# A decoder layer on one core: transposes of q, k and dequantised weight rows taken from TensorE and given to VectorE and the stores

## The chip, the core and the metric

The kernel runs on one core of a Trainium2 chip, in one launch. Its time is the device time in microseconds (us), the median of several runs. TensorE is called PE in the profile (PEld is its weight load), VectorE DVE, ScalarE ACT, GpSimd POOL, and SyncE, which here only issues DMAs, SP.

## The reference

A post-norm decoder layer over 8 batches of 256 tokens, width 1024, float32. Each of three sublayers is added to its input and normalised.

```python
# 1: causal attention, 32 heads of 32, 8 key/value heads
qkv = x @ w_qkv
xq, xk = rope(xq), rope(xk)          # pairs (x1, x2) -> (x1 cos - x2 sin, x1 sin + x2 cos)
probs = softmax(mask(xq @ xk.T / sqrt(32)));  out = (probs @ xv) @ w_o
# 2: cross-attention to ctx_4096, one head of 1024
Q = h @ Wq.T + bq;  K = ctx @ Wk.T + bk;  out = softmax(Q @ K.T / 32) @ ctx
# 3: a linear layer whose weight is dequantised: 4 (or 8) bit planes -> code -> table row
w_l = take_along_axis(lut4, code4, axis=1);  w_h = take_along_axis(lut8, code8, axis=1)
y = where(norm(x) > 64, x @ w_h.T, x @ w_l.T) + bias
```

## The kernel before, in words

All work is in tiles of 128 partitions. Most matrix products run as seven block products per batch (`winograd`), with the sums of blocks made by DVE or POOL. The program has three stages, and on PE, DVE, ACT and POOL every instruction keeps the order in which the Python code issues it (class `InOrder`; all of them carry line 59 in the profile). DMAs written as `nc.sync.dma_start` go to SP's one queue in an order that a scheduler sets when the kernel is built, those written as `sync.dma_start` in the order of the program.

**Stage 1 (`front(b)`, lines 581 to 675).** For each batch, q (four accumulators of 128 tokens x 512 columns) and k, v (256 columns each) are multiplied. A loop over steps (28 for a batch, 32 for the first) sets the order: one half product a step, q and k/v in turn. A finished accumulator is handed to `rotate` (line 543): four DVE multiplications over the even or the odd elements write `ra` and `rb`, POOL adds them (line 559), and five steps later `turn` (line 561) transposes `ra` on PE in 128x128 blocks into a PSUM bank (tag `tp`, two banks) and ACT copies the bank into `q_t` or `k_t`, q scaled by 1/sqrt(32). At the end of a batch q_t, k_t and v are stored to DRAM (`keep_q`, `keep_kv`).

**The dequantisation (`dequant_low`, line 340)** is a generator beside this, 64 blocks of 128 rows x 128 columns, five steps each. In a block DVE masks bit plane 0 (`first`) and makes it 0 or 1, masks planes 1 to 3 (`m`); ACT makes eight leaves `t` out of the table; DVE selects between them in three predicated copies, the last two of them one block later (`finish`), and the 128x128 result is stored to `wr_d`, 64 stores. Line 661 sets how many of the 320 steps are done in stage 1: 240. The others are done in stage 2, three in a visit.

**Stage 2 (lines 678 to 922).** 48 visits, six a batch, and three more to drain: scores, softmax and values of a group of heads, in portions, PE work of four different visits overlapping (`LAG = 3`). Beside the visits, four portions in each, runs a chain of other work (`Beside`): the output projection of the batch before (15 steps), the product of the two cross-attention weights (`weight_product`, 24 pieces of two steps, which begins at the end of stage 1), and in batches 5 and 6 `weights_turned(4)`, 8 steps each: `transpose_weights` (line 402) loads rows of `wr_d` (tile `row`), PE transposes them, ACT copies the bank to `stage`, and a store writes `wf_d`. `run(low)` (line 891, visit 33) finishes the dequantisation. In its last eight pieces `weight_product` also stores a column of 128 single elements to `u_d`, loads a row block of wk into `wide` (tag `row`, two buffers, shared with the rows above) and reduces it on DVE (line 472). The tag `m` (two buffers) is shared by the pieces' results and `stage`.

**Stage 3 (lines 926 to 1115).** Cross-attention and the linear layer; it loads `wf_d` in four quarters (`quads`, line 261) when the last projection lets go of the buffers.

Of the kernel before, what the change touches and what calls it, by code (L numbers as in the profile page):

```python
# [24 lines left out]
F32 = mybir.dt.float32  # L25
BF16 = mybir.dt.bfloat16
I32 = mybir.dt.int32
# [35 lines left out]
def decoder_layer(  # L63
# [67 lines left out]
    wr_d = dram.tile([KC, P, D], F32, name="wr_d")  # L131
    wf_d = dram.tile([2, 2, P, 4, 512], F32, name="wf_d")
    u_d = dram.tile([D], F32, name="u_d")
# [127 lines left out]
    def quads(pool, src, tag, width=512):  # L261

        t = [pool.tile([P, 4, width], F32, name=f"{tag}{i}", tag=f"{tag}{i}") for i in range(7)]
        for i in (0, 2, 1, 3):
            sync.dma_start(t[i], src[i // 2, i % 2])
        return t
# [72 lines left out]

    def dequant_low(pool, bits, lut, width=P):  # L340


        words = width // 32
        last = None

        def finish(n):
            if last is None:
                return
            t, m, to = last
            if n == 1:  # L350
                select(t, m[:, 0:1, :], 1)
            else:
                select(t, m[:, 1:2, :], 2)
                select(t, m[:, 2:3, :], 3)
                nc.sync.dma_start(to, t[:, 0, :])

        for oi in range(KC):
            qw, lt = table(pool, oi, 4, lut, 2)
            diff = pool.tile([P, 8], F32, tag="diff", name="diff", bufs=2)
            dve.tensor_tensor(diff, lt[:, :, 1], lt[:, :, 0], ALU.subtract)  # L360
            for i in range(0, D, width):
                part = slice(i // 32, i // 32 + words)
                first = pool.tile([P, 1, words, 32], I32, tag="first", name="first")
                first = planes_of(qw[:, 0:1, part], bits, first)
                first = first[:, 0]
                one = first.bitcast(F32)
                dve.tensor_scalar(one, first, 0, None, ALU.not_equal)
# [12 lines left out]
                yield  # L380
                finish(2)
                last = t, m, wr_d[oi, :, i : i + width]
                yield
        finish(1)
        finish(2)
# [42 lines left out]
    def weight_product():  # L428
        bq_bc = m_pool.tile([P, D], F32, name="bq_bc")
        nc.sync.dma_start(bq_bc, bq.partition_broadcast(P))  # L430
        wide = dq.tile([P, D], F32, tag="row", name="wide", bufs=2)
        nc.sync.dma_start(wide, bk.partition_broadcast(P))
# [15 lines left out]
        for k, (n, i) in enumerate(pieces):  # L448
# [13 lines left out]
            if k + 2 < len(pieces):  # L462
                loaded.append(load(*pieces[k + 2]))
            m = m_pool.tile([P, 512], F32, tag="m", name="m", bufs=2)[:, :third]
            act.copy(m, ps)
            nc.sync.dma_start(m_d[i, :, ts(n, third)], m)
            if n == 2:
                u = D - 2 * third
                nc.sync.dma_start(u_d[ts(i, P)].rearrange("(p o) -> p o", o=1), m[:, u : u + 1])
                wide = dq.tile([P, D], F32, tag="row", name="wide", bufs=2)  # L470
                nc.sync.dma_start(wide, wk_t[ts(i, P), :])
# [18 lines left out]
    def low_steps(n):  # L490
        for _ in range(n):
            next(low, None)

    def put_low(oi, tp, half):
        stage = m_pool.tile([P, 512], F32, tag="m", name="stage", bufs=2)
        act.copy(stage, tp)
        to = wf_d[half, oi // 4, :, :, ts(oi % 4, P)]
        nc.sync.dma_start(to, stage.rearrange("p (q o) -> p q o", q=4))

    low_turned = transpose_weights(dq, put_low)  # L500


# [30 lines left out]

    cs = f_pool.tile([P, NST, 48], F32, name="cs", bufs=1)
    nc.sync.dma_start(cs, rope.rearrange("(s p) a -> p s a", p=P))
    for i in (1, 3):
# [4 lines left out]
    nc.sync.dma_start(bits, bit)  # L541

    def rotate(acc, st, jn, to):

        n = HD * 4 * jn
        pairs = acc[:, :n].rearrange("p (r j i two) -> p r j i two", r=4, j=jn, two=2)

        order = "p (j r i two) -> p r j i two" if jn == 4 else "p (r j i two) -> p r j i two"
        ra = f_pool.tile([P, n], F32, tag=f"ra{jn}", name="ra", bufs=3 if jn == 4 else 2)
        rb = f_pool.tile([P, n], F32, tag=f"rb{jn}", name="rb", bufs=1)  # L550
        pa, pb = (t[:, :n].rearrange(order, r=4, j=jn, two=2) for t in (ra, rb))
        cos, nsin, sin = (
            cs[:, st : st + 1, None, ts(i, 16)].to_broadcast([P, 4, jn, 16]) for i in range(3)
        )
        dve.tensor_tensor(pa[..., 0], pairs[..., 0], cos, ALU.mult)
        dve.tensor_tensor(pa[..., 1], pairs[..., 1], cos, ALU.mult)
        dve.tensor_tensor(pb[..., 0], pairs[..., 1], nsin, ALU.mult)
        dve.tensor_tensor(pb[..., 1], pairs[..., 0], sin, ALU.mult)
        pool_e.tensor_tensor(ra[:, :n], ra[:, :n], rb[:, :n], ALU.add)

        def turn():
            tp = bank(p_tp, "tp")
            for j in range(jn):
                transpose(tp[:, ts(j, P)], ra[:, ts(j, P)], ident)
            tp = tp[:, :n].rearrange("p (j s) -> p j s", j=jn)

            act.mul(to, tp, 1.0 / HD**0.5 if jn == 4 else 1.0)

        later.append((step + 5, turn))
# [11 lines left out]
    def front(b):  # L581
        n_kv = NKV * HD
        k_t = f_pool.tile([P, 2, S], F32, tag="k_t", name="k_t", bufs=1)
        v = f_pool.tile([P, NST, NKV * HD], F32, tag="v", name="v", bufs=1)
        q_t = [f_pool.tile([P, 4, S], F32, tag=f"q_t{jb}", name="q_t", bufs=1) for jb in range(2)]
        acc = {}
# [11 lines left out]
        def finish_q(st, half):  # L598
            rotate(acc[st, half], st, 4, q_t[half][:, :, ts(st, P)])

        def put_kv(st, half, ps):
            n = NKV * HD
            if half:
                act.copy(v[:, st, :], ps[:, :n])
                return
            acc[st] = f_pool.tile([P, n], F32, tag="acc_k", name="acc_k")
            act.copy(acc[st][:, :n], ps[:, :n])
            if st == 1:
                rotate(acc[st], st, 2, k_t[:, :, ts(st, P)])

        def add_kv(st, half, ps):
# [3 lines left out]
            if not half:  # L615
                rotate(acc[st], st, 2, k_t[:, :, ts(st, P)])

# [5 lines left out]
        def whole_kv(st, half, ps):  # L623
            put_kv(st, half, ps)
            if (st, half) == (0, 0):
                rotate(acc[0], 0, 2, k_t[:, :, :P])

        def keep_q():
            for jb in range(2):
                nc.sync.dma_start(q_d[b][jb], q_t[jb])  # L630

        def keep_kv():
            nc.sync.dma_start(k_d[b], k_t)
            nc.sync.dma_start(v_d[b], v)

        def kept(steps, keep):
            yield from steps
            later.append((step + 5, keep))

# [4 lines left out]
        else:  # L644
# [3 lines left out]
            kv_steps = classical(p1, a, (raw_kv[0:2], raw_kv[2:4]), n_kv, whole_kv, "uv")  # L648
        yield from in_turn(kept(q_steps, keep_q), kept(kv_steps, keep_kv))

# [4 lines left out]
    for b in range(B):  # L655
        for n, _ in enumerate(front(b), 1):
# [3 lines left out]

            while low_done * (steps - 20) < 240 * (step - 20):
                low_steps(1)
                low_done += 1
# [8 lines left out]
    for _, f in later:  # L672
        next(product)
        f()
    s1_stack.close()

# [137 lines left out]

    def weights_turned(n):
        for _ in range(2 * n):
            next(low_turned, None)
            yield

    mw = []  # L820
# [48 lines left out]
    for k in range(len(visits) + LAG):  # L869
# [14 lines left out]
        if k >= EACH and k % EACH == LAG and b < B:  # L884
# [5 lines left out]
            if b == 5:  # L890
                run(low)
            if 5 <= b <= 6:
                parts.append((weights_turned(4), 8))
            beside = Beside(4 * EACH, *parts)
# [264 lines left out]
def _rope_table(np):  # L1159
# [5 lines left out]
    cos, sin = np.cos(angles), np.sin(angles)  # L1165
    return np.concatenate([cos, -sin, sin], axis=1).astype(np.float32)

# [53 lines left out]
```

## Time and profile before

| | us |
|---|---|
| median of 3 runs | 1531.33 (1527.86 to 1533.06) |
| the profiled execution, its own time | 1527.34 |
| its span, first to last instruction | 1525.3 |
| busy: PE / DVE / ACT / POOL | 1407.2 / 993.7 / 661.6 / 510.3 |
| mean granted TensorE clock | 0.979 |
| DMA | 69755 packets, 153.06 MB; 12944 packets under 512 B |

The profile is one execution. A row of a table of stretches gives, for a stretch of the span, each engine's busy time with its number of instructions, the granted TensorE clock (1.00 is full speed), the mean busy share of the 16 DMA engines and GB/s. A row of waits gives the engine and tile that waited, what ended the wait, and the total time, the number and the longest. A row of a tile gives the shortest, median and longest duration of its instructions in ns. In a timeline, a row is a start, a length, an engine and an operation, with the number of instructions merged into it.

### The profile page before, as it was taken

How to read it: one execution, taken by the hardware profiler on the slowest of the kernel's cores; microseconds unless marked ns; L12 is line 12 of the kernel's file. 1: busy time of each engine (PE TensorE's matmuls, PEld its weight loads, DVE VectorE, ACT ScalarE, POOL GpSimd, SP SyncE). 2: the span in 40 equal slices, each digit the busy share in tenths (PEclk: the TensorE clock that was granted, in tenths of full speed). 3: DMA queues.
4: the chain of work that ended last, by engine and by line, in shares of the span. 5: the costliest groups of instructions: out<-in, count | busy, mean ns of one | idle time of the engine just before them, and what ended most of it. 6: DMA issues, size and time to landing. Idle time of an engine off the chain costs nothing. (4 is left out here: it accounts for less than half of the span.)

```text
span 1525.3 us, 20159 instructions
## 1 busy us (share of the span) xinstructions
PE 1407.2 (92%) x7314; PEld 884.5 (58%) x7314; DVE 993.7 (65%) x1579; ACT 661.6 (43%) x2028; POOL 510.3 (33%) x304
## 2 busy tenths in 40 slices
PE   8899899898899999989979789999999999999996
PEld 4555555555455555455545444885867667685842
DVE  3977778683988889987655674345455464545462
ACT  1556566662688787776545662012111011202110
POOL 2623323220745354443424352064133131404112
PEclk9999999999999999999988999999999999999999
DMA  9222112215641216061463345421222122131211
GB/s 332 74 82 84 57 39 89 81 52 194 237 174 62 100 42 159 24 152 58 104 145 100 115 135 195 150 84 42 98 77 89 56 83 69 70 111 39 73 41 44
DMA packets 69755, 153.06 MB, mean 100 GB/s; under 512 B 12944, under 2 KB 32400, under 8 KB 67216
## 3 DMA queue, kind: packets, MB, share of 16 engines
q1 hardware_dynamic: 69648, 151.70, 30.7%
q8 instruction: 60, 0.98, 0.3%
q14 instruction: 47, 0.39, 0.1%
HBM read 101.33 MB, written 50.34 MB: 99 GB/s over the span
## 5 line engine op out<-in xcount | busy, mean ns | idle before, releaser
L59 POOL TENSOR_TENSOR pr<-pr,rsum 128x1024 f32<-128x1024 f32 x96 | 187.3, 1952 | 284.7 <-DVE rsum L59 246.0
L59 ACT ACTIVATE t<-first,lt,diff 128x128 f32<-128x128 f32 x512 | 206.0, 483 | 98.4 <-DMA wr_d<-t 45.5
L59 ACT ACTIVATE pr<-pr,nm 128x256 f32<-128x256 f32 (+1 forms) x512 | 226.0, 446 | 41.0 <-DVE rsum L59 22.3
L59 DVE COPY_PREDICATED t<-m,t 128x512 f32<-128x512 int32 (+2 forms) x192 | 156.1, 813 | 3.2
L59 PEld LDWEIGHTS tp<-ident,pr 128*128 128x128 f32 x800 | 94.1, 143 | 106.2 <-issue 77.0
L59 PE MATMUL tp<-ident,pr 128*128 128x128 f32 x800 | 125.2, 284 | 25.8 <-ACT pt L59 19.3
L59 DVE TENSOR_TENSOR pr<-sc,causal 128x1024 f32<-128x1024 f32 x96 | 115.9, 1208 | 48.3 <-PE sc L59 34.3
L59 POOL TENSOR_TENSOR ra<-ra,rb 128x512 f32<-128x512 f32 (+1 forms) x48 | 63.7, 1327 | 242.4 <-DVE rb L59 238.8
L59 DVE TENSOR_REDUCE nm<-pr 128x4 f32<-128x1024 f32 (+1 forms) x96 | 117.1, 1220 | 3.3
L59 PE MATMUL x<-wq,xt 128*128 128x512 f32 x200 | 98.9, 618 | 16.9 <-ACT acc L59 10.3
L59 ACT COPY pt<-tp 128x512 f32<-128x512 f32 (+1 forms) x144 | 74.7, 554 | 79.3 <-PE tp L59 79.2
L59 POOL TENSOR_TENSOR sf<-h_t 128x512 f32<-128x512 f32 x8 | 10.2, 1271 | 288.1 <-DVE h_t L59 275.7
L59 ACT ACTIVATE sd<-mv,eps 128x1 f32<-128x1 f32 (+2 forms) x34 | 10.0, 295 | 220.9 <-DVE mv L59 220.9
L59 ACT ACTIVATION_READ_ACCUMULATOR pr<-pr,nm 128x1 f32 x512 | 97.6, 191 | 0.0
L59 PE MATMUL x<-w,o_t 128*128 128x512 f32 x192 | 89.7, 594 | 0.8 <-DVE h L59 0.8
L59 DVE TENSOR_TENSOR h<-x,h 128x512 f32<-128x512 f32 x64 | 44.0, 687 | 65.7 <-PE x L59 58.1
L59 PE MATMUL x<-w,h_t 128*128 128x512 f32 x192 | 86.3, 592 | 0.0
L59 ACT COPY h_t<-tp 128x512 f32<-128x512 f32 x32 | 18.7, 584 | 128.6 <-PE tp L59 128.6
L59 PE MATMUL tp<-pt,v 128*32 128x256 f32 (+1 forms) x640 | 63.2, 435 | 10.9 <-DVE pt L59 5.6
L59 DVE TENSOR_TENSOR h<-z,h 128x512 f32<-128x512 f32 x48 | 33.0, 687 | 59.0 <-PE z L59 57.6
L59 DVE COPY pt<-tp 128x512 f32<-128x512 f32 x64 | 43.2, 676 | 43.1 <-PE tp L59 43.0
L59 PE MATMUL x<-wk,wq 128*128 128x342 f32 x192 | 62.1, 469 | 6.0 <-ACT t L59 4.1
(144 smaller groups left out, 2741.1 us busy)
## 6 DMA issues: line engine op xcount, KB each, us to landing
h_d<-h SPq DMA_DIRECT2D x32, 512.0 KB, 3.4
wq<-in_wq SPq DMA_DIRECT2D x24, 512.0 KB, 5.2
xt<-in_x_t SPq DMA_DIRECT2D x32, 256.0 KB, 4.4
q_d<-q_t SPq DMA_DIRECT2D x16, 512.0 KB, 3.1
q_t<-q_d SPq DMA_DIRECT2D x16, 512.0 KB, 6.0
h<-in_x SPq DMA_DIRECT2D x16, 512.0 KB, 6.7
h<-h_d SPq DMA_DIRECT2D x16, 512.0 KB, 4.0
ct_b<-in_c_t SPq DMA_DIRECT2D x8, 1024.0 KB, 4.8
```

The costliest lines, as they stand in the source:

```text
L59: return lambda *args, **kw: self.tc.keep_in_program_order(issue(*args, **kw))
```

## The change

`rotate` makes two wide multiplications on DVE, over a table that holds each cosine and sine twice (a reversed read swaps the pairs), and a scaled table `cs_q` takes the place of the scaling on ACT. POOL adds as before. `turn` is a DVE transpose, which transposes each 32x32 square of the tile by itself into `turned` (two buffers), and four stores, one for each group of 32 partitions, place the squares in `q_d` or `k_d` in runs of 32 floats (128 B). The tiles q_t and k_t of stage 1 and their stores at the end of a batch are gone.

In the dequantisation, the plane 0 mask is made for two blocks at once; a finished block is transposed in squares by DVE, and after every second block four stores place the squares in `wf_d`, whose layout gets the group of 32 as an inner dimension. `wr_d`'s use for this, `put_low`, `weights_turned` and its loads, PE transposes and copies are gone. 210 steps are done in stage 1 where 240 were. `wide` has one buffer, `m` is as wide as its pieces, and the four loads of `wf_d` are sixteen, of 32 partitions each.

```diff
-    wf_d = dram.tile([2, 2, P, 4, 512], F32, name="wf_d")
+    wf_d = dram.tile([2, 2, 32, 4, 4, 512], F32, name="wf_d")
...
+            for c in range(4):
+                sync.dma_start(t[i][ts(c, 32)], block[:, :, c])
...
-                nc.sync.dma_start(to, t[:, 0, :])
+                oi, i = to
+                if i % 256 == 0:
+                    rows.append(pool.tile([P, 2, 4, 32], F32, tag="turned", name="turned", bufs=2))
+                dve.transpose(rows[-1][:, i // P % 2].rearrange("p c o -> p (c o)"), t[:, 0, :])
+                if i % 256:
+                    q = i // P % 4 - 1
+                    for a in range(4):
+                        o = P * (oi % 4) + 32 * a
+                        nc.sync.dma_start(
+                            wf_d[i // 512, oi // 4, :, q : q + 2, :, o : o + 32],
+                            rows[-1][32 * a : 32 * a + 32],
+                        )
...
-                first = pool.tile([P, 1, words, 32], I32, tag="first", name="first")
+                if i % 256 == 0:
+                    first = pool.tile([P, 1, 8, 32], I32, tag="first", name="first")
...
-        wide = dq.tile([P, D], F32, tag="row", name="wide", bufs=2)
+        wide = dq.tile([P, D], F32, tag="row", name="wide", bufs=1)
...
-        dve.tensor_tensor(pa[..., 0], pairs[..., 0], cos, ALU.mult)
-        dve.tensor_tensor(pa[..., 1], pairs[..., 1], cos, ALU.mult)
-        dve.tensor_tensor(pb[..., 0], pairs[..., 1], nsin, ALU.mult)
-        dve.tensor_tensor(pb[..., 1], pairs[..., 0], sin, ALU.mult)
+        dve.tensor_tensor(ra.rearrange(order, r=4, j=jn), heads, cos, ALU.mult)
+        dve.tensor_tensor(
+            rb.rearrange("p (h i two) -> p h i two", i=16, two=2),
+            swapped,
+            sin.rearrange("p h (i two) -> p h i two", two=2),
+            ALU.mult,
+        )
...
         def turn():
-            tp = bank(p_tp, "tp")
-            for j in range(jn):
-                transpose(tp[:, ts(j, P)], ra[:, ts(j, P)], ident)
-            tp = tp[:, :n].rearrange("p (j s) -> p j s", j=jn)
-            act.mul(to, tp, 1.0 / HD**0.5 if jn == 4 else 1.0)
+            turned = f_pool.tile([P, n], F32, tag=f"turned{jn}", name="turned", bufs=2)
+            dve.transpose(turned, ra)
+            for a in range(4):
+                rows = slice(HD * a, HD * a + HD)
+                at = slice(P * st + HD * a, P * st + HD * a + HD)
+                nc.sync.dma_start(
+                    to[:, :, at].rearrange("(r d) j s -> d j r s", r=4),
+                    turned[rows].rearrange("d (j r s) -> d j r s", j=jn, r=4),
+                )
...
-            while low_done * (steps - 20) < 240 * (step - 20):
+            while low_done * (steps - 20) < 210 * (step - 20):
...
-            if 5 <= b <= 6:
-                parts.append((weights_turned(4), 8))
```

More of the change, by code (lines that the diff above doesn't have):

```diff
@@ L264, in quads @@
         for i in (0, 2, 1, 3):
-            sync.dma_start(t[i], src[i // 2, i % 2])
+            block = src[i // 2, i % 2]
+            if block.shape[0] == P:
+                sync.dma_start(t[i], block)
+                continue
+            for c in range(4):
+                sync.dma_start(t[i][ts(c, 32)], block[:, :, c])
         return t
@@ L336, in table, with dequant_low @@
         return qw, lt
-    def dequant_low(pool, bits, lut, width=P):
-        words = width // 32
+    def dequant_low(pool, bits, lut):
+        width, words = P, P // 32
         last = None
@@ L354, in finish @@
                 select(t, m[:, 2:3, :], 3)
-                nc.sync.dma_start(to, t[:, 0, :])
+                oi, i = to
[10 more added lines that the diff above has]
+                        )
+        rows = []
         for oi in range(KC):
@@ L362, in dequant_low @@
                 part = slice(i // 32, i // 32 + words)
-                first = pool.tile([P, 1, words, 32], I32, tag="first", name="first")
[L364 to L367, printed above, removed]
+                if i % 256 == 0:
+                    first = pool.tile([P, 1, 8, 32], I32, tag="first", name="first")
+                    first = planes_of(qw[:, 0:1, i // 32 : i // 32 + 8], bits, first)[:, 0]
+                    ones_of = first.bitcast(F32)
+                    dve.tensor_scalar(ones_of, first, 0, None, ALU.not_equal)
+                one = ones_of[:, i % 256 : i % 256 + width]
                 yield
@@ L381, in dequant_low @@
                 finish(2)
-                last = t, m, wr_d[oi, :, i : i + width]
+                last = t, m, (oi, i)
                 yield
@@ L463, in weight_product @@
                 loaded.append(load(*pieces[k + 2]))
-            m = m_pool.tile([P, 512], F32, tag="m", name="m", bufs=2)[:, :third]
+            m = m_pool.tile([P, third], F32, tag="m", name="m", bufs=2)
             act.copy(m, ps)
@@ L469, in weight_product @@
                 nc.sync.dma_start(u_d[ts(i, P)].rearrange("(p o) -> p o", o=1), m[:, u : u + 1])
-                wide = dq.tile([P, D], F32, tag="row", name="wide", bufs=2)
+                wide = dq.tile([P, D], F32, tag="row", name="wide", bufs=1)
                 nc.sync.dma_start(wide, wk_t[ts(i, P), :])
@@ L492, in low_steps @@
             next(low, None)
[L494 to L500, printed above, removed]
     s1_stack = ExitStack()
@@ L532, in decoder_layer @@
     )
-    cs = f_pool.tile([P, NST, 48], F32, name="cs", bufs=1)
+    cs = f_pool.tile([P, NST, 2 * HD], F32, name="cs", bufs=1)
     nc.sync.dma_start(cs, rope.rearrange("(s p) a -> p s a", p=P))
+    cs_q = f_pool.tile([P, NST, 2 * HD], F32, tag="cs_q", name="cs_q", bufs=1)
     for i in (1, 3):
@@ L541, in decoder_layer @@
     nc.sync.dma_start(bits, bit)
+    dve.tensor_scalar(cs_q, cs, 1.0 / HD**0.5, None, ALU.mult)
     def rotate(acc, st, jn, to):
         n = HD * 4 * jn
-        pairs = acc[:, :n].rearrange("p (r j i two) -> p r j i two", r=4, j=jn, two=2)
-        order = "p (j r i two) -> p r j i two" if jn == 4 else "p (r j i two) -> p r j i two"
+        heads = acc[:, :n].rearrange("p (r j d) -> p r j d", r=4, j=jn)
+        swapped = acc[:, :n].rearrange("p (h i two) -> p h i two", i=16, two=2)[..., ::-1]
+        order = "p (j r d) -> p r j d" if jn == 4 else "p (r j d) -> p r j d"
@@ L549, in rotate @@
         ra = f_pool.tile([P, n], F32, tag=f"ra{jn}", name="ra", bufs=3 if jn == 4 else 2)
         rb = f_pool.tile([P, n], F32, tag=f"rb{jn}", name="rb", bufs=1)
-        pa, pb = (t[:, :n].rearrange(order, r=4, j=jn, two=2) for t in (ra, rb))
-        cos, nsin, sin = (
-            cs[:, st : st + 1, None, ts(i, 16)].to_broadcast([P, 4, jn, 16]) for i in range(3)
-        )
-        dve.tensor_tensor(pa[..., 0], pairs[..., 0], cos, ALU.mult)
-        dve.tensor_tensor(pa[..., 1], pairs[..., 1], cos, ALU.mult)
@@ L557, in rotate @@
-        dve.tensor_tensor(pb[..., 0], pairs[..., 1], nsin, ALU.mult)
-        dve.tensor_tensor(pb[..., 1], pairs[..., 0], sin, ALU.mult)
-        pool_e.tensor_tensor(ra[:, :n], ra[:, :n], rb[:, :n], ALU.add)
-        def turn():
-            tp = bank(p_tp, "tp")
-            for j in range(jn):
-                transpose(tp[:, ts(j, P)], ra[:, ts(j, P)], ident)
-            tp = tp[:, :n].rearrange("p (j s) -> p j s", j=jn)
-            act.mul(to, tp, 1.0 / HD**0.5 if jn == 4 else 1.0)
+        angles = cs_q if jn == 4 else cs
@@ new lines, in rotate @@
+        cos = angles[:, st : st + 1, None, 0:HD].to_broadcast([P, 4, jn, HD])
+        sin = angles[:, st : st + 1, HD:].to_broadcast([P, 4 * jn, HD])
+        dve.tensor_tensor(ra.rearrange(order, r=4, j=jn), heads, cos, ALU.mult)
[4 more added lines that the diff above has]
+            ALU.mult,
+        )
+        own = ra.rearrange(order, r=4, j=jn)
+        pool_e.tensor_tensor(own, own, rb.rearrange("p (r j d) -> p r j d", r=4, j=jn), ALU.add)
@@ L582, in front @@
         n_kv = NKV * HD
-        k_t = f_pool.tile([P, 2, S], F32, tag="k_t", name="k_t", bufs=1)
         v = f_pool.tile([P, NST, NKV * HD], F32, tag="v", name="v", bufs=1)
-        q_t = [f_pool.tile([P, 4, S], F32, tag=f"q_t{jb}", name="q_t", bufs=1) for jb in range(2)]
         acc = {}
@@ L598, in finish_q @@
         def finish_q(st, half):
-            rotate(acc[st, half], st, 4, q_t[half][:, :, ts(st, P)])
+            rotate(acc[st, half], st, 4, q_d[b][half])
         def put_kv(st, half, ps):
@@ L608, in put_kv @@
             if st == 1:
-                rotate(acc[st], st, 2, k_t[:, :, ts(st, P)])
+                rotate(acc[st], st, 2, k_d[b])
         def add_kv(st, half, ps):
@@ L615, in add_kv @@
             if not half:
-                rotate(acc[st], st, 2, k_t[:, :, ts(st, P)])
+                rotate(acc[st], st, 2, k_d[b])
         def whole_q(st, half, ps):
@@ L625, in whole_kv, with keep_v, kept @@
             if (st, half) == (0, 0):
[L626 to L633, printed above, removed]
+                rotate(acc[0], 0, 2, k_d[b])
+        def keep_v():
             nc.sync.dma_start(v_d[b], v)
-        def kept(steps, keep):
+        def kept(steps):
             yield from steps
-            later.append((step + 5, keep))
+            later.append((step + 5, keep_v))
         if b:
@@ L648, in front @@
             kv_steps = classical(p1, a, (raw_kv[0:2], raw_kv[2:4]), n_kv, whole_kv, "uv")
-        yield from in_turn(kept(q_steps, keep_q), kept(kv_steps, keep_kv))
+        yield from in_turn(q_steps, kept(kv_steps))
     at = dict(zip(((0, 18), (0, 22), (0, 28), (0, 31)), [(w1q_sums, 1)] * 4))
@@ L674, in decoder_layer @@
         f()
+    if len(later) % 2:
+        next(product)
     s1_stack.close()
@@ L813, in project @@
         yield
[L815 to L818, printed above, removed]
     mw = []
@@ L1165, in _rope_table @@
     cos, sin = np.cos(angles), np.sin(angles)
-    return np.concatenate([cos, -sin, sin], axis=1).astype(np.float32)
+    pairs = (np.stack(two, axis=2).reshape(S, HD) for two in ((cos, cos), (-sin, sin)))
+    return np.concatenate(list(pairs), axis=1).astype(np.float32)
 def kernel(**inputs):
```

## The prediction, made before the changed kernel was run

> **What bounds the kernel now.** I read the page's busy times first: which engine has no room.
>
> ```profile
> PE 1407.2 (92%) x7314; PEld 884.5 (58%) x7314; DVE 993.7 (65%) x1579; ACT 661.6 (43%) x2028; POOL 510.3 (33%) x304
> ```
>
> PE is the bound over the whole, so work taken from it can count. But shares are averages; next the table of stretches, by stage.
>
> ```profile
> core 0: us, PE busy (x) PEld busy (x) DVE busy (x) ACT busy (x) POOL busy (x), PEclk, DMA share, GB/s
> ...
> 45.00:345.00 300.00, 278.31 (x922) 163.55 (x921) 239.29 (x484) 183.28 (x458) 95.98 (x69) 0.98 0.21 69
> ...
> 372.00:778.00 406.00, 375.65 (x2415) 214.38 (x2416) 342.10 (x449) 290.54 (x1058) 187.70 (x97) 0.99 0.38 118
> 778.00:820.00 42.00, 28.83 (x191) 18.23 (x190) 16.28 (x20) 19.78 (x65) 12.60 (x8) 0.76 0.75 160
> ...
> 855.00:885.00 30.00, 20.88 (x169) 13.80 (x168) 17.47 (x25) 19.36 (x68) 12.68 (x8) 0.77 0.51 150
> ...
> 932.00:1525.00 593.00, 565.84 (x2970) 398.70 (x2970) 295.16 (x489) 80.85 (x162) 151.62 (x87) 0.99 0.23 84
> ```
>
> Stage 1 (to about 360 us) and most of stage 2 have PE near 93% with DVE at 80 to 84%. Two stretches are different: 778 to 820 and 855 to 885, where PE is busy for 69% and its clock is down to 0.76. Both are where rows of `wr_d` are transposed. The change touches stage 3 only in a load. So I asked who ends PE's waits in stage 1, then in 778 to 885.
>
> ```profile
> PE x L59 <- ACT acc L59: 10.3, 3, 4.0
> PE tp L59 <- POOL ra L59: 9.2, 11, 4.5
> PE u L59 <- ACT acc_k L59: 2.1, 1, 2.1
> ```
>
> ```profile
> PE tp L59 <- ACT stage L59: 9.7, 6, 4.3
> PE tp L59 <- DMA row<-wr_d: 5.6, 1, 5.6
> ```
>
> The first three are all of PE's idle time in stage 1; 9.2 us of it is PE waiting to transpose a rotated tile. The last two are the row transposes.
>
> **Part A, stage 1: the rotation.** What do PE's transposes cost? Not 278 ns each, the mean duration in the page's kind of row: they overlap. The timeline gives starts:
>
> ```profile
> 343.10 1.88 PE L59 MATMUL z<-wq,sx 128*128 128x512 f32 x4
> 344.81 0.60 PE L59 MATMUL tp<-ident,ra 128*128 128x128 f32 x4
> 345.25 0.60 PE L59 MATMUL v<-wkv,sx 128*128 128x256 f32 x2
> ```
>
> From the four transposes' start to the next product's is 0.44 us, 0.11 us each. There are 160 in stage 1 (8 batches x (4 x 4 of q + 2 x 2 of k)): 17.6 us of pure PE time go. The waits on `ra` go with them: 9.2 us in this stretch. ACT loses 32 copies of 592 ns and 16 of 384 ns (25 us in sum), and its 38 us of waits for the store that frees `t`, since DVE's transpose now reads `t`; so I expect half of the 10.3 us of ACT's late copies to go, 5 us. Together 32 us.
>
> Against that, what DVE gets. A q rotation has four multiplications of 421 ns = 1.68 us. After: two of 128x512, for which the row of `acc<-z,acc` (128x512) shows 0.68 us, and a transpose. No transpose on DVE is in the trace. The nearest row is that same one, 0.68; the lower bound is a half of it, the upper twice. The Trainium skill ("Vector Engine (DVE) Microarchitecture Reference", 3.8) says the 32x32 array sustains one element per cycle per lane, which points to the row's figure: I take 0.69. Then 2.06 us against 1.68, +0.38 x 32 = +12 us. A k rotation: four at some 0.37 (means 0.43 and 0.31) = 1.47 before, three of 128x256 at 0.42 = 1.26 after, -3 us. Dequantisation: a 128x128 transpose at 0.29 a block (128 is a quarter of 512: 0.13 us and the fixed 0.15 of 0.42 - 0.27), and some 0.35 saved by masking plane 0 for two blocks at once (0.45 + 0.44 us a block now): nothing net. But 30 steps leave stage 1, six blocks; one costs DVE 168 us / 45 = 3.7 us here, so -22 us. DVE in stage 1 ends about 13 us lower, at some 86% of a shorter stage: not the bound. If a transpose takes 1.4 us, it is 22 + 8 + 10 = 40 us more, and DVE is.
>
> A rule speaks against this part: "VectorE: DVE Perf Modes" (Rules for kernel authors) sends a 128x128 transpose to TensorE where PSUM may receive it. By it the sum would be 0.44 us of PE bought with 0.69 of DVE, a loss. By the rows, PE's 0.44 us also carries a wait (9.2 us over 41 additions) and an ACT copy of 0.59, and DVE is the engine with room. I go with the rows, for the wait.
>
> Now the stores: the q rotation's single share of a 512 KB store becomes four DMAs of 512 packets of 128 B. In a batch: 4 x 4 + 2 x 4 = 24 DMAs with 10,240 packets, and 2.6 pairs of blocks with 4 DMAs of 256 packets each, 2,690 more: 12,900 packets, 808 an engine. "DMA: Bandwidth & Descriptors" (Specifications) says a transfer wants 512 B at least, below which the engine reads, modifies and writes; by it I would put 128 B at no less than a 512 B packet. What the trace has, in the table of stretches: loads of `qw` in 128 B packets, and a `wr_d` store in 512 B packets.
>
> ```profile
> 92.10:92.80 0.70, 0.70 (x3) 0.32 (x2) 0.68 (x1) 0.70 (x3) 0.08 (x1) 1.00 0.60 94
> 121.90:122.30 0.40, 0.40 (x2) 0.16 (x2) 0.00 (x0) 0.40 (x2) 0.00 (x0) 1.00 0.57 164
> ```
>
> 512 packets within 0.70 us are 22 ns a packet and engine; 128 within 0.40 are at most 50, about 41 from first to last. So 128 B written lies between 20 ns (like the read) and 41 ns (like a whole 512 B): 16 to 33 us of a batch's some 40 us. I take 25 ns, 20 us: with the 4 us of the other transfers it fits, and costs waits only. SP issues 34 DMAs in place of 8: at 0.45 us (0.38 for `qw`, 0.52 for the `stage` store) 15 us of 40, also within. The DVE transpose newly waits for its buffer: the four stores of two rotations ago, 2 us of issue and 3 us to land, while q rotations come 5 to 10 us apart. Behind it on DVE stand the accumulator additions that free PE's banks, and `first`, for which ACT waits. SP's in-order wait for DVE holds back the next batch's `xt` as the waits for `t` do now (181 us in all). I charge 7 us for both. At the stage's end the last k goes through four DMAs, not one: 1 us. Three deferred items and one extra step again make four steps of `product`, so its pieces stay where they were.
>
> A: 32 - 7 - 1 = 24 us gained; bounds 5 (new waits replace the old) and 37.
>
> **Part B, stage 2: rows.** The two strange stretches last 72 us. Work in them at full clock: 28.83 x 0.76 + 20.88 x 0.77 = 38 us, less 64 transposes x 0.11 = 7: 31 us, which at the neighbours' 96% and 0.99 takes 33 us. So up to 39 us. The floor is what bears the name: 9.7 + 5.6 of waits and 7 of transposes, 22 us. Nothing else late stands there except the slow DMAs behind `u_d`, which stay: I take 35.
>
> **Part C, one buffer for `wide`.** Here a wait is added.
>
> ```profile
> L59 DVE CUSTOM_DVE_ANT_0 wide<-wide,bq_bc x9: 1172/1215/1220, 252.4 to 782.3; 128x1024 f32<-128x1024 f32 x9
> L471 SPq DMA_DIRECT2D wide<-in_wk_t x8: 332/333/632, 28.3 to 731.9; - x8
> ...
> DMA to landing us min/median/max: 3.3/10.6/13.5
> ```
>
> The timeline has these reductions in four pairs: at 596.2 and 601.6, 663.5 and 668.3, 725.7 and 730.6, 776.4 and 782.3. With two buffers each was loaded a pair ahead and nobody waited. With one, the second's load can leave only after the first reduction, at 597.5, 664.7, 726.9, 777.5. DMAs that left at the first three times landed after 12.2, 9.3 and 10.5 us, because a store of single elements to `u_d` (11.2 us median) stands just before; the fourth I put at 11. So DVE, in order, would stand still for 8.1, 5.7, 6.8 and 6.2 us. Behind it: the reciprocals for POOL, and the additions that free the four banks of scores PE needs next. PE holds some 4 us of other work, but DVE is 95% busy in 572 to 672 and can't catch up. I charge 17 us of the 27; bounds 0 (quick landing) and 30 (PE's clock falls with its idle time).
>
> **Part D, later dequantisation.** 210 + 33 x 3 = 309 steps are done before visit 33; `run(low)` then does the last 12 of 321 in one lump: 2.4 blocks, 9 us of ACT (8 x 0.48 a block) and as much of DVE, in front of that visit: 4 us of PE. Six more visits carry dequantisation: PE is busy 91.2 of 100 us in 572 to 672 against 102.7 of 106 after it, so 5.7% of 66 us, 4 us. D: 8 us lost (3 to 12). The sixteen loads of `wf_d` cost SP some 5 us; the last of four left at 955.6 and POOL used them at 1001.5, so 30 us of cover hide it. If that were gone, 5 us.
>
> Sum against the profiled execution: 24 + 35 - 17 - 8 = 34 us off a span of 1525.3: 1491. The median is 6.0 above that span (2.0 around it, 4.0 between executions): 1497.
>
> **Rivals.** *The `wide` loads land in time* (5 us): C is nothing, 1480. For it: the `row` loads that shared the queue are gone. Against: the first pairs had no row load near and still took 9 to 12 us. *PE's saved time in stage 1 turns into DVE's or SP's waits*: A is 5, 1516, up to 1526 with C at 30. For it: DVE at 86%, in order, with single PSUM banks. *The other side: stores bind stage 1.* A batch's 808 packets an engine plus 4 us exceed its 39 us from 43 ns a packet on, just above the upper bound. At 60 ns a batch takes 52 us instead of 43, 8 batches +70 us; with -35, +17, +8 that is 1590; at 50 ns, near 1525 to 1540. Every packet would show it; the 22 ns read speaks against, the 512 B rule for it. The work does what it says in any case: the PE transposes are gone from the program.
>
> **Numbers.** Forecast 0.50 (1478 to 1515), `wide` in time 0.20 (1462 to 1482), stage 1 gives nothing 0.18 (1512 to 1528), stores bind 0.12 (1530 to 1600). Measuring tells some 0.3% from no change, 4.6 us: so faster has 0.84 (the first two and most of the third), within 0.3% 0.04, slower 0.12. Range 1464 to 1526, leaving out the slow case and the ends.
>
> **What would show it.** Right: no `tp<-ident,ra` and `tp<-ident,row`; a DVE transpose of 128x512 near 0.69 us; stage 1 over near 335 us with PE at 96%; no stretch with a clock of 0.76 near 780; DVE waiting for DMA `wide` four times, 5 to 8 us each. Wrong: DMA share near 1.0 through stage 1, DVE or SP waiting for `turned`; transposes over 1 us.

## The result, and the profile after

The changed kernel takes 1509.3 us (median of 4 runs, 1508.0 to 1511.6) against 1532.2 us beside it: ratio 0.9857, 95% interval 0.9833 to 0.9881. It is faster by 22.9 us, where 34 were forecast; 1509.3 lies inside the range. Its profiled execution spans 1508.4 us, 16.9 us less than before's 1525.3. The working below is in spans and starts of visits, which compare one profiled execution with another; where a part's worth is given in medians, it says so.

The page's busy times of the changed kernel:

```profile
PE 1386.5 (92%) x7090; PEld 863.2 (57%) x7090; DVE 1005.2 (67%) x1532; ACT 632.4 (42%) x1964; POOL 508.2 (34%) x304
```

224 instructions and 21 us of TensorE's busy time are gone. The share is 92% still, so shares say nothing of where the time went. The stretches do (columns as before; stage 1 now ends earlier, hence 325):

```profile
45.00:325.00 280.00, 265.52 (x800) 153.32 (x799) 244.21 (x416) 150.78 (x379) 99.81 (x70) 0.98 0.39 74
372.00:778.00 406.00, 356.62 (x2281) 200.23 (x2274) 335.07 (x460) 293.83 (x1045) 176.00 (x94) 0.95 0.34 91
778.00:820.00 42.00, 34.35 (x222) 19.62 (x220) 24.87 (x37) 22.87 (x87) 16.10 (x10) 0.92 0.58 187
855.00:885.00 30.00, 25.18 (x184) 13.97 (x186) 23.61 (x34) 21.32 (x83) 17.31 (x12) 0.94 0.17 54
```

Stage 1 is denser (TensorE 95% of it, from 93), with DMA at 0.39, not near 1. The clock of 0.76 near 780 and 0.77 near 855 is gone. But 372 to 778, where nothing was to be repaired, fell from 375.65 busy us to 356.62 and from a clock of 0.99 to 0.95: some of the gain was lost there. What the new operations cost, by groups (0 to 372 us) and by one store's line:

```profile
L59 DVE STREAM_TRANSPOSE turned<-ra 128x512 f32<-128x512 f32 x32 | 22.4, 700 | 0.0
L59 DVE STREAM_TRANSPOSE turned<-t 128x128 f32<-128x128 f32 x41 | 12.8, 311 | 1.4
```

```profile
L588 SPq DMA_DIRECT2D q_d<-turned x128: 569/627/3293, 32.0 to 334.2; - x128
...
DMA to landing us min/median/max: 1.9/2.2/8.5
```

0.70 us for a 128x512 transpose and 0.31 for 128x128, as taken (0.69 and 0.29). A store of 64 KB in 128 B packets costs SyncE 0.63 us and lands after 2.2.

The best single ruler is when the scores of each attention visit begin, read off the trace. (Each experiment's ratio is to the kernel before measured beside it, whose medians lie between 1528.4 and 1531.7 us, so differences of medians between experiments are uncertain by some 3 us.) Each kernel's starts, less those of the kernel before (us; minus is earlier; A rotation, B rows, C one buffer for `wide`, 210 or 240 the pace):

```
kernel                          visit 0    21      33      34      47
changed (A, B, C, 210)           -28.3   -25.4    -8.7    +6.3   -16.1
  wide in two halves             -27.4   -27.9   -24.5   -13.0   -45.2
  u column gathered              -28.8   -27.9   -20.3    -9.2   -35.5
  two halves, 240                -14.1   -13.0   -12.3   -14.0   -45.5
  two halves, no lump            -30.3   -30.6   -27.3   -27.5   -57.3
  two halves, no lump, gathered  -31.3   -31.8   -28.4   -28.6   -56.5
  two halves, gathered, 240      -12.1   -12.8   -12.1   -13.8   -45.2
A alone, 240                     +13.4   +18.0   +18.0   +18.0   +17.4
A alone, third t                 -12.4    -9.5    -9.5    -9.5   -10.6
A, 210                            +0.7    +1.5    +6.4   +25.1   +23.4
B alone, 240                      -2.0    -3.2    -2.5    -4.2   -35.9
B, 210, no lump                  -12.3   -10.8    -7.1    -7.3   -36.2
C alone                           +0.6    +1.7   +16.8   +24.7   +21.8
```

First row: 25 us won in stage 1, nearly all lost between visits 21 and 34, then 22 won net. The five kernels that have A, B and 210 reach visit 21 25.4 to 31.8 us ahead: stage 1 differs by some 3 us either way from one profile to the next, and smaller differences are not read.

### The profile page after: what moved, and what is told of

It reads as the page before. It is cut to its first block, busy times and chain, and to the rows that moved or that the text cites. A ratio compares the mean times of both kernels' runs of the same rounds, so it can differ in the third digit from the quotient of the medians.

```text
span 1508.4 us, 19847 instructions
## 1 busy us (share of the span) xinstructions
PE 1386.5 (92%) x7090; PEld 863.2 (57%) x7090; DVE 1005.2 (67%) x1532; ACT 632.4 (42%) x1964; POOL 508.2 (34%) x304
## 4 chain that ended last, share of the span: by engine, by line
PE 61%; DVE 19%; ACT 9%; DMA 5%; issue 3%; POOL 0%; SPq 0%; ACTq 0%; DVEq 0%; POOLq 0%
PE x L59 24%; PE z L59 18%; PE tp L59 8%; DVE nm L59 4%; ACT pr L59 4%; PE cross L59 4%; DVE t L59 3%; PE u L59 3%; DMA wide<-in_wk_t 3%; DVE pr L59 2%; DVE uh L59 2%; ACT t L59 2%; PE sc L59 2%; PE v L59 2%; DVE pt L59 2%
## 5 line engine op out<-in xcount | busy, mean ns | idle before, releaser
L59 DVE COPY_PREDICATED t<-m,t 128x512 f32<-128x512 int32 (+2 forms) x192 | 161.1, 839 | 4.7 <-ACT t L59 1.8
L59 POOL TENSOR_TENSOR ra<-ra,rb 128x512 f32<-128x512 f32 (+1 forms) x48 | 57.4, 1196 | 208.9 <-DVE rb L59 177.8
L59 PE MATMUL tp<-pt,v 128*32 128x256 f32 (+1 forms) x640 | 70.0, 446 | 34.0 <-DVE pt L59 31.0
L59 PE MATMUL x<-w,o_t 128*128 128x512 f32 x192 | 94.4, 618 | 0.8 <-DVE h L59 0.8
L59 ACT COPY o_t<-tp 128x256 f32<-128x256 f32 (+1 forms) x48 | 21.2, 442 | 110.1 <-PE tp L59 110.1
```

The lines of the kernel that those rows point to most:

```text
L59: return lambda *args, **kw: self.tc.keep_in_program_order(issue(*args, **kw))
```

## The experiments

**1. The wait for `wide`.** Theory: the four waits that one buffer adds cost all their length and more. The rivals: the forecast's share of it, or nothing. One kernel takes the waits away; the second adds them, alone, to the kernel before.

```
-                wide = dq.tile([P, D], F32, tag="row", name="wide", bufs=1)
+                if i == 0:
+                    spare = m_pool.tile([P, KC, third], F32, tag="wk", name="wide", bufs=2)
+                    spare = spare.rearrange("p k c -> p (k c)")
+                wide = spare[:, ts(i % 2, D)]
```

> The changed kernel with the single buffer of wide undone: the eight wk_t rows take turns in two halves of a wk buffer that is idle by then, so nothing else moves. Theory now (the four waits of VectorE cost their 23 us of waiting and some more, since TensorE's clock falls after each): 26 us less than the changed kernel, 1483. As the prediction charged it (17 of the 27 us on the path): 1492. Rival (the waits stand beside a backlog of VectorE that would be there anyway): under 5 us, 1505 or more. In the trace the waits of DVE for DMA wide should be gone, and visits 22 to 40 should start about as far ahead of the kernel before as visit 21 does (25 us).

> The kernel before with one buffer for the eight wk_t rows (one half of an idle wk buffer, reused each time), the rest untouched: part C alone. Theory: 26 us more than before, 1558. As charged in the prediction: 17 more, 1549. Rival (a backlog hides it): under 5 more, 1537 or less. In the trace DVE should wait for DMA wide four times, 5 to 8 us each.

Two halves: 1483.2 us, ratio to before 0.9692 (0.9668 to 0.9715), 26 us less than the changed kernel. One half alone in the kernel before (`ts(0, D)` each time): 1549.8, ratio 1.0131 (1.0108 to 1.0155), 21 us more. So C costs 21 to 26 us, not 17. The timeline of the changed kernel shows one wait; in brackets is the idle time before an instruction and what ended it:

```profile
570.67 1.22 DVE L59 CUSTOM_DVE_ANT_0 wide<-wide,bq_bc 128x1024 f32<-128x1024 f32 x1
...
571.93 0.33 SPq L492 DMA_DIRECT2D wide<-in_wk_t  x1
...
575.52 0.68 DVE L59 COPY pt<-tp 128x512 f32<-128x512 f32 x1
...
581.91 1.23 DVE L59 CUSTOM_DVE_ANT_0 wide<-wide,bq_bc 128x1024 f32<-128x1024 f32 x1 [5.62 <-DMA wide<-in_wk_t]
583.07 0.69 DVE L59 COPY pt<-tp 128x512 f32<-128x512 f32 x1
...
583.81 0.18 PEld L59 LDWEIGHTS tp<-pt,v 128*32 128x32 f32 x2 [7.39 <-DVE pt L59]
```

The load leaves when the first reduction is over, VectorE stands still for 5.62 us, and behind the second reduction stands a copy of `pt`, for which TensorE's weight load stood idle 7.39 us. VectorE's whole bill is in its waits, and the load's time to landing in the tile's row:

```profile
DVE wide L59 <- DMA wide<-in_wk_t: 22.8, 4, 6.7
...
DMA to landing us min/median/max: 3.7/8.5/10.4
```

Four waits, as forecast; 22.8 us, not 26.8. How 22.8 us of VectorE become 26 of the whole is seen from the start of visit 21 to that of visit 45, first in the changed kernel, then in the one with two halves:

```profile
574.30:864.70 290.40, 244.63 (x1537) 131.93 (x1536) 214.70 (x307) 189.06 (x686) 110.98 (x64) 0.94 0.35 88
571.80:836.20 264.40, 234.45 (x1537) 128.15 (x1536) 221.71 (x307) 188.76 (x686) 115.81 (x64) 0.98 0.35 95
```

The stretch is 26.0 us longer. TensorE is idle in it (length less busy time) for 45.8 us against 30.0, 15.8 more, and it is busy for 10.2 us longer with the same 1537 instructions, at a clock of 0.94 against 0.98. So TensorE had other work for part of the waits (15.8 of 22.8 us reached it), and the rest is the lower clock. C alone in the kernel before shows the same two parts: 302.0 us against 282.0 between these visits, 15.9 more idle and 4.2 more busy. The clock falls right behind each wait. First the changed kernel, then the one with two halves, around the first two waits:

```profile
571.00:591.00 20.00, 12.73 (x73) 6.65 (x72) 11.75 (x19) 8.21 (x27) 8.60 (x6) 0.83 0.90 139
646.00:666.00 20.00, 14.59 (x77) 7.43 (x76) 12.87 (x22) 8.70 (x31) 9.39 (x6) 0.83 0.93 147
```

```profile
571.00:591.00 20.00, 18.30 (x122) 9.02 (x120) 18.70 (x24) 14.19 (x53) 12.76 (x8) 1.00 0.74 95
646.00:666.00 20.00, 17.02 (x99) 8.77 (x97) 16.51 (x23) 15.68 (x59) 10.72 (x7) 1.00 0.22 44
```

Around the first wait TensorE was busy for 12.7 us of 20 at a clock of 0.83, against 18.3 at 1.00. The second half of that stretch in the changed kernel, behind the wait:

```profile
581.00:591.00 10.00, 7.19 (x18) 3.25 (x19) 6.52 (x9) 4.17 (x14) 2.33 (x2) 0.66 0.65 97
```

**2. Why `wide` lands late.** Theory: the eight stores of single elements to `u_d` hold up the load behind them. The kernel keeps one buffer and takes those stores away.

```
-                nc.sync.dma_start(u_d[ts(i, P)].rearrange("(p o) -> p o", o=1), m[:, u : u + 1])
+                act.copy(u_c[:, i : i + 1], m[:, u : u + 1])
...
+        if k == 45:
+            run(product)
+            tp = bank(p_tp, "tp")
+            transpose(tp[:KC, :P], u_c, ident)
+            act.copy(u_r, tp[:KC, :P])
+            nc.sync.dma_start(u_d.rearrange("(k p) -> k p", p=P), u_r)
```

> The changed kernel, one buffer for wide kept, without the eight stores of single elements to u_d: ScalarE copies each column into a 128x8 tile, which TensorE transposes once near 860 us for one store of 8 rows. Theory (those stores hold up the loads of wk_t that leave just behind them): the loads land in some 4 us, not 8 to 10, DVE's four waits for DMA wide fall from 23 us to under 10, time 1490 to 1495. Rival (a load of 512 KB needs 8 to 10 us there anyway): waits stay near 23 us, 1505 to 1510.

1488.3 us, ratio 0.9736 (0.9714 to 0.9758): 21 of the 26 us come back by the medians, 17 between visits 21 and 45 (273.0 us against 290.4), with the single buffer still there. The tile `wide` in this kernel:

```profile
  DVE wide L59: 5.4, 4
...
DMA to landing us min/median/max: 3.2/4.7/7.2
```

The same 512 KB load lands in 4.7 us, where the changed kernel's took 8.5 (median). The rival, that such a load needs 8 to 10 us, is out. The buffer and the stores are two halves of one cost: either repair takes most of it.

**3. The lump and the pace.** `run(low)` is put off to visit 39 (`b == 6`), and in another kernel the pace is put back to 240; both with `wide` in two halves.

> The changed kernel with wide in two halves, and the rest of dequantisation run at visit 39, not 33, so that the last 12 steps go three to a visit as before and there is no lump. Theory (the lump costs 11.5 us at visit 33 and the four visits that take it cost 1 to 3): 1473 to 1475. Rival (the work costs the same wherever it is put): 1483.

> The changed kernel with wide in two halves and dequantisation at the old pace of 240: parts A and B alone. In the run with the pace of 210 the lump before visit 34 cost 11.5 us of a lead of 24.5. If the later dequantisation is only a cost (as the prediction has it, 8 us): 1472 to 1475. If the 30 steps that left stage 1 are what lets the new rotation fit there (VectorE at 244 of 280 us would go to 266): first scores at 362 or later instead of 351, and 1483 to 1495. I lean to the middle, 1480.

Without the lump: 1471.3 us, ratio 0.9624 (0.9606 to 0.9642), 11.9 less than with it. The lump is seen in the stretches from 706 to 731 of the kernel that has it, and from 703 to 729 of the one that has not (visits 33 and 34 start 24.6 us apart in the first, 12.9 in the second):

```profile
706.00:718.00 12.00, 8.05 (x60) 3.63 (x58) 11.25 (x19) 7.22 (x19) 5.74 (x3) 1.00 0.92 196
718.00:731.00 13.00, 7.28 (x20) 3.79 (x20) 9.13 (x15) 10.21 (x37) 5.02 (x4) 0.61 0.12 20
```

```profile
703.00:716.00 13.00, 12.11 (x77) 6.15 (x75) 12.83 (x20) 11.17 (x38) 9.50 (x6) 1.00 0.83 186
716.00:729.00 13.00, 11.73 (x94) 5.99 (x92) 12.05 (x14) 10.37 (x37) 6.28 (x4) 1.00 0.01 3
```

TensorE is busy for 15.3 us of 25 and its clock is down to 0.61. With the old pace: 1482.4, the same as with the new pace and its lump (1483.2). Visits 21 and 33 say why: the old pace loses 15 us in stage 1 (13.0 ahead, not 27.9), the new one 3.4 us in the denser visits to 33 and 11.5 in the lump. So the pace is worth 15 us to stage 1 (19 with the column gathered), a gain that the prediction does not book. It is seen in TensorE's waits for the copies by which ScalarE empties its banks. In the kernel with two halves and 240 (45 to 345 us):

```profile
PE x L59 <- ACT acc L59: 18.1, 4, 6.6
PE u L59 <- ACT acc_k L59: 9.4, 2, 6.7
```

With two halves and 210 the same rows have 7.2 and 3.7.

**4. The rotation alone.** A, in the kernel before, with nothing else.

> The kernel before with the rotation part alone: two wide multiplications, VectorE's transposes of q and k and their stores; rows, dequantisation, its pace of 240 and wide's two buffers as before. Theory (part A, 24 us forecast, 25 to 28 read off the starts of visits): 1507. Rival (new waits for VectorE eat the saved time; the 25 us come from the 30 steps of dequantisation that left stage 1, not from the rotation): 1525 to 1530. In the trace, first scores at 350 us by the theory, at 370 by the rival.

1547.3 us, ratio 1.0121 (1.0099 to 1.0142): slower by 19 us, beyond what either theory allowed. The waits of stage 1 (45 to 345 us) in this kernel:

```profile
ACT t L59 <- DMA wr_d<-t: 85.0, 24, 10.5
...
PE x L59 <- ACT acc L59: 29.2, 6, 7.0
```

In the kernel before these are 38.0 and 10.3. ScalarE may not overwrite `t` before its store to `wr_d` is done. SyncE issues in order, and four stores of each rotation now stand there, waiting for VectorE (56 us at that line). A `wr_d` store lands 1.8 us after it leaves, nearly as before (1.6), which speaks for its leaving late. Behind ScalarE's wait stand the copies that free TensorE's banks. If that is so, a third buffer for `t` must help:

```
+                if (D * oi + i) // P < 40 and (D * oi + i) // P % 3 == 2:
+                    t = f_pool.tile([P, 8, width], F32, tag="t", name="t", bufs=1)
+                else:
+                    t = pool.tile([P, 8, width], F32, tag="t", name="t", bufs=2)
```

> The rotation alone again, but with a third buffer for t in stage 1 (blocks 2, 5, 8 and so on up to 39 take it), so that ScalarE needs the store of the block three back, not two. Theory (the rotation's stores stand before the wr_d stores in SyncE's queue, wait there for VectorE, and ScalarE waits for wr_d before it can free TensorE's banks): most of the 18 us lost in stage 1 come back, first scores at 375 or earlier, 1522 to 1530. Rival (VectorE's transposes and the 128 B stores themselves cost the time): first scores at 388 or later, 1542 or more.

1517.0 us, ratio 0.9925 (0.9907 to 0.9942), 30 less than without it; first scores 26 us earlier. The same waits:

```profile
PE x L59 <- ACT acc L59: 21.2, 4, 6.2
...
ACT t L59 <- DMA wr_d<-t: 16.3, 7, 4.8
```

The transposes and 128 B stores are all still there, so the rival that they are the cost is out: the wait of `t` for its store is. More came back than the 18 us that A had lost, and no run gives the kernel before a third `t` without the rotation; what the buffer would win there stays open.

What A does to TensorE is seen from 45 us to the first scores. The rows are the kernel before, A alone, A alone with a third `t`, and the changed kernel:

```profile
45.00:378.70 333.70, 306.71 (x1018) 181.02 (x1016) 249.19 (x506) 193.57 (x483) 99.38 (x72) 0.97 0.25 83
45.00:392.10 347.10, 299.10 (x866) 171.81 (x864) 258.45 (x462) 173.25 (x438) 97.75 (x72) 0.92 0.36 76
45.00:366.30 321.30, 289.98 (x868) 168.80 (x866) 261.34 (x462) 173.31 (x438) 98.27 (x72) 0.95 0.39 82
45.00:350.40 305.40, 287.29 (x868) 166.82 (x866) 250.85 (x427) 155.79 (x391) 101.92 (x72) 0.97 0.42 86
```

Busy time times clock gives TensorE's work as 298, 275, 275 and 279 us: the rotation takes some 20 us from it in every kernel. Its idle time is 27.0, 48.0, 31.3 and 18.1 us. Alone, the rotation buys its 20 us with 21 of idle time and a lower clock.

**5. What rescues the rotation in the changed kernel.** Rows alone, rotation with the new pace, and rows with the new pace (two halves and no lump in both kernels with rows).

> The kernel before with the dequantised rows alone: transposed on VectorE in stage 1 and 2, placed by their stores, no row loads and row transposes in stage 2; rotation as before, pace 240, wide in two halves of an idle buffer. As the prediction had it (part B): 35 us less than before, 1497. As the starts of visits after 33 read (16 + 3 + 5 us): 24 less, 1508. Rival (stage 1 pays for it, VectorE having more there with the old rotation): 1520 or more.

> The rotation alone with the new pace of 210, rows as before (the lump at visit 33 stays, since the rows are turned from there on): parts A and D. If the pace is what rescues the rotation: first scores near 366 us, as with the rows at the old pace, or earlier. If the rows are, because VectorE's transpose frees t where the store to wr_d did: first scores at 375 or later, and ScalarE still waits over 60 us for wr_d in stage 1. I lean to the second; the time then 1530 to 1545 with the lump's some 12 us.

> The rows alone with the new pace of 210, wide in two halves and no lump: parts B and D, with the old rotation. Against the run with all of these and the new rotation (1471; first scores at 348) it gives what the rotation is worth when the other parts are there. If the pace by itself eases stage 1 (VectorE behind in either case): first scores near 365, and the rotation is worth 15 us or less. If TensorE's transposes bind it as the prediction has it (17.6 us of TensorE's time, and the waits for POOL): first scores at 370 or later, the rotation worth over 20, 1492 or more.

B alone: 1493.7, ratio 0.9783 (0.9755 to 0.9811; six runs, 1490.5 to 1502.0), 35 us less in medians; 33 of them after visit 33, where the rows were transposed. A with 210: 1553.4, ratio 1.0157 (1.0135 to 1.0179); stage 1 ends 1.5 us behind the kernel before and ScalarE waits 85.9 us for `wr_d`, so the pace makes good A's loss of 18 but brings no gain, and here the lump costs 19 us. (The time was expected at 1530 to 1545.) B with 210: 1487.1, ratio 0.9720 (0.9700 to 0.9739), between the two theories: the rotation is worth 15.8 us by the medians (against 1471.3), 19.8 by visit 21 (the profile of B with 210 is that of its slowest run). At 240 it is worth 11.4 and 9.8. With the rows, `t` is freed by VectorE's transpose and the store to `wr_d` is gone. ScalarE's wait for `t` in the changed kernel (45 to 325 us), where A alone has 85.0:

```profile
ACT t L59 <- DVE turned L59: 37.4, 10, 9.4
```

So the rotation pays with the rows, as it did with a third `t`; with the pace alone it does not.

**6. All repairs together.**

> The changed kernel with all three repairs: wide in two halves, the u column gathered and stored as 8 rows, no lump at visit 33. If the stores of single elements held up nothing but the wk_t rows: 1471, as the run with two halves and no lump. If they also held up the loads of wq (TensorE waited 9 us for those in the run with two halves): 1463 to 1468. I lean to 1467.

> The changed kernel with wide in two halves, the u column gathered, and dequantisation at the old pace of 240 (which leaves no lump either). By the two runs of the pace so far (15 us lost in stage 1 by the old pace, 3 us lost by the dense visits of the new one): 11 or 12 us above the same kernel at 210, 1478 to 1480. Rival (the gathered column gives VectorE time that makes the old pace fit): within 4 us of it.

1472.6 us (ratio 0.9625, 0.9606 to 0.9644), no less than with two halves and no lump (1471.3): the `u_d` stores cost nothing once `wide` has two buffers, and my lean to 1467 was a miss. At 240: 1482.3 (0.9680, 0.9666 to 0.9695), 10 us more. So the best version is the changed kernel with `wide` in two halves and no lump: 38 us under the changed kernel by the medians, 36 by the ratios, and 58 under the kernel before.

## Where the prediction held and where it failed

The sum by its own parts, in the changed kernel's span: stage 1 won 25.4 (visit 21), and the rows 32 (visits 34 to 47 of the kernel with two halves, 45.2 - 13.0); C cost 26 (by the medians, and by visit 47: 29.1 against two halves, less the 2.5 by which stage 1 differs) and the later dequantisation 15 in stage 2 (11.5 + 3.4). 25.4 + 32 - 26 - 15 = 16, and the span fell by 16.9; 34 had been written. Of the shortfall C makes 9 us, D 7 and B 3; A is 1 over. The medians differ by 6 more, since before's profiled span was 6.9 below its median and the changed one's 0.9.

- **B, 35 us: right.** 33 in stage 2 and 35 by medians alone. The estimate from "work at full clock against the neighbours' share" held, not the 22 us of named waits.
- **C, 17 us: the largest error, a term of the sum put at nothing.** The times of the reductions, the count and the place were right (forecast 8.1, 5.7, 6.8, 6.2; 26.8 in sum; measured 22.8). "I charge 17 us of the 27" was right too for what it counts, TensorE's idle time: 15.8. What it leaves out is the clock behind each wait, 10 us more here and 4 with C alone. The prediction named it ("PE's clock falls with its idle time"), but only for its upper bound of 30, which was close.
- **D, the other mis-sized term: "8 us lost".** The lump was put at 4 us of TensorE's time; it took 11.5, more than the 9 us of ScalarE's work in it. The denser visits were put at 4 and took 3.4. Missing was the other sign: the 30 steps were said to keep VectorE off the bound, and were worth 15 us in stage 1. So D as a whole is nothing (1483.2 against 1482.4).
- **A, 24 us: the terms right in this kernel, but not as the rotation's own.** Durations, "no `tp<-ident,ra`", TensorE at 95% (96 forecast) and a DMA share far from 1 are as forecast. So is much of the sum: some 20 us of work taken from TensorE (17.6 forecast), the 9.2 us of waits on `ra` gone, ScalarE's late copies from 10.3 us down to 7.2 (45 to 345 us). New waits of TensorE are some 3 us (27.0 - 9.2 - 3.1 leaves 14.7, and it is idle for 18.1), where 7 were charged. But the same 20 us are taken in A alone, which loses 18 by new waits. That they stay small in the changed kernel is owed to two other edits: the rows, which free `t` (the prediction says "since DVE's transpose now reads `t`" under A; that is B's edit), and the pace. That 24 was met is in part luck. Two readings failed: ScalarE's 38 us of waits for `t` did not go, they are 37.4 and now end with VectorE; and VectorE's work did not fall by 13 us (249.2 before, 250.9 after, to the first scores), in part since its predicated copies took longer (of 128x512 0.81 before, 1.00 after; why, no run shows).
- **A sign named as wrong came true.** SyncE waited for `turned` in stage 1, 47.4 us at the stores of q and k and 27.2 at those of the rows (45 to 325 us). Stage 1 gained all the same; in the kernel before SyncE waited 181.2 us for `t` there.
- **The rule against A** ("VectorE: DVE Perf Modes", Rules for kernel authors: a 128x128 transpose belongs on TensorE if PSUM may take it) comes out for the rotation alone, +19 us, and not with a third `t`, -12, nor with the rows and the pace, -16. A transpose of 128x512 took VectorE 0.70 us in all of them, so its price did not decide; what the stores stood in front of did.
- **The rivals.** `wide` in time: out. Stores bind: out, and its bounds were misread: the 22 ns a packet are the length of a stretch in which the DMA engines were busy for 0.60 of the time, which is 13 ns. Stage 1 gives nothing (1516) is nearer in time than the forecast's 1497, but its mechanism occurred only where the rotation stands without the rows (A alone, A with 210); in the changed kernel stage 1 gave all that was forecast, and stage 2 took it.

Argued and not shown: that SyncE's order is what delays `wr_d` rests on its waits and on the landing time; the order itself was not changed in any run.

## What to carry to other kernels

When an in-order engine gets a wait in a stretch where the engine it feeds is 90% busy, charge the idle time that reaches the fed engine (here 16 us of 23) and, as a second term, its lower clock afterwards (here 10 us more). Then ask what makes the transfer late: here a second buffer, or taking away the small stores ahead of it, was worth about as much as the whole change. Before booking a gain to an edit, ask which other edit makes it possible: stores added to an in-order queue can delay every buffer that another store on that queue must free. Work put off to "run the rest here" costs what its engines need plus the clock that the starved engine loses, so spread it.

## What the runs showed of the hardware that was not expected

- 128 B packets written are not dear. By the packet records of the changed kernel, 118,912 of them took 13 ns each in the mean, as the 128 B reads of the kernel before did (12.9), and less than the lower bound of 20 that the prediction read. The prediction took "DMA: Bandwidth & Descriptors" (Specifications: below 512 B the engine reads, modifies and writes) to put them at a 512 B packet or more; a 512 B packet took 28 ns in the kernel before, so no sign of that is seen here.
- Eight stores of 128 single elements each, some 4 KB in all, nearly doubled the landing time of the 512 KB loads behind them (8.5 against 4.7 us) and so, with one buffer, cost 17 to 21 us.
- The granted clock falls within the same 10 to 20 us in which TensorE is starved: 0.66 behind a wait for `wide`, 0.61 in the lump, 1.00 in the same stretch without them. Over four waits this made the same TensorE instructions 10 us longer.
